# Layer 3's softmax totals in a four-layer graph-attention kernel: weights added up by fours on DVE, with one group of tile matmuls per head

## The chip, the cores and the metric

The kernel runs on one core of a Trainium2 chip. The metric is the device time of one launch, in microseconds (us), as a median over runs. The engines are named as in the profile: PE (TensorE matmul), PEld (its weight loads), DVE (VectorE), ACT (ScalarE), POOL (GpSimd) and SP (SyncE, which here issues DMAs). Each engine works through its own queue in order; where an instruction needs the result of another engine, it waits for a semaphore.

## The reference

There are 16 batches of 1024 nodes with 256 features, in fp32, and a 0/1 adjacency matrix per batch. Four attention layers follow one another. Each adds its result to x:

```python
h = jnp.maximum(_layernorm(x, axis=-1), 0.0)
x = x + _L3_gnn_ref(h, adj, ...)          # layers 0 to 2 likewise
```

Each layer projects h with a weight matrix, builds a 1024 x 1024 matrix of weights from two scores per node (masked by the adjacency), and takes the weighted mean of the projected values: the sum of weight times value over the source nodes, divided by the sum of the weights. Layer 3 does so with 4 heads of 64 features each, and then normalizes every head:

```python
dst = jnp.einsum('bhij,bhje->bhie', attention, h) + bias[None, :, None, :]
out = jax.nn.relu(dst) + h
out = (out - mu) / jnp.sqrt(var + EPS) * ln_gamma[...] + ln_beta[...]
```

The divisor of the softmax, one number per target node and head, is what the change computes in another way. It is called the total below.

## The kernel before, in words

**Streams.** The kernel keeps two batches under way. `stream(0)` runs the even batches, `stream(1)` the odd ones. Both are Python generators that emit instructions and yield planned times; the loop at the end of `short_path` always advances the stream whose planned time is behind, and stream 1 starts with a lag of 111 planned units. The order in which instructions are emitted is their precedence. A scheduler then fixes each engine's queue: where an instruction isn't ready by the scheduler's own account, a later one that is ready may go ahead. `keep_in_program_order` and `high_priority` pin some of them.

**A block** is 128 nodes; a batch has 8 (NI). Pairs of blocks are normalized and projected in `project`: the shifted relu (`center_by_sums`, L302, on DVE) makes `centered`, PE transposes it (L338), ACT copies it out (L340), PE multiplies with W (L345), and an evict function writes the values V (L413 to L417). The variance comes from a Square with accumulation on ACT (L309).

**Weights.** `weigh` fills a row of 1024 scores in PSUM by PE (L374 or L574) and makes for each source block j one 128 x 1024 tile of weights on DVE (L367), masked by the adjacency. A stream has 8 buffers for these tiles, and the two streams share the one row in PSUM.

**Layers 0 to 2** (`attend`) multiply with the weights as the stationary operand: for a target block, 8 matmuls over the source blocks into one accumulator of 257 columns (L461), whose last column is the total. `finish` then updates x_b (L385 to L397, or L501) on DVE and ACT.

**Layer 3** turns this around. The values of one head (64 columns, as two slices of 32) and a column for the total are the stationary operand, the weights of 512 targets the moving one. Each matmul uses a column tile of 32 (QUAD) columns of PE, and four of them, in four column tiles, make a group (`in_tiles`, L586). In `add_values` a source block takes four matmuls: two halves of the targets by two slices. In `add_totals` a pair of source blocks takes four: two halves by two blocks, with the total's column (E) broadcast to 32 columns. So a head has 32 matmuls for values and 16 for totals. Every fp32 matmul stands as two records in the trace, so these are 64 and 32 records. While head h is multiplied, DVE makes the weights of head h + 1.

After a head, ACT copies the two accumulators (L663), PE turns them (L670, L678), DVE takes the inverse of the totals and writes y (L672, L681). `center` (L544 to L556) adds the bias, relu and h3, and removes the mean; `rescale` (L560 to L562) multiplies with the inverse root of the variance and gamma and adds x. y is a buffer of its own, 8 KB per partition, from which the output is sent.

The lines that do the totals before:

```python
parts = [
    (V3[:, j + n, h, E:].to_broadcast([P, QUAD]), halves_of(h, j + n)[g])
    for g, n in ((0, 1), (0, 0), (1, 1), (1, 0))
]
in_tiles(parts, total, j == 2, j == NI - 4)
```

Of the kernel before, what the change touches and what calls it, by code (L numbers as in the profile page):

```python
# [41 lines left out]
P = 128  # L42
# [19 lines left out]
def short_path(ctx: ExitStack, tc: tile.TileContext, ins: dict, out: bass.AP, bad: bass.AP):  # L62
# [233 lines left out]
    def accumulator(b: int) -> bass.AP:  # L296
        return psum.tile([P, HALF], F32, name=f"acc{b % 2}")

    def center_by_sums(xb: bass.AP, minus_mean: bass.AP, pair: int, centered: bass.AP) -> bass.AP:

        for n in range(2):
            nc.vector.tensor_scalar(  # L302
                centered[:, n, :], xb[:, 2 * pair + n, :], minus_mean[:, n : n + 1], 0.0,
                op0=ALU.add, op1=ALU.max,
            )
        squared = small.tile([P, 2], F32, name="squared")
        for n in range(2):
            square = work.tile([P, D], BF, name="square", bufs=1)
            nc.scalar.activation(  # L309
                square, xb[:, 2 * pair + n, :], AF.Square, bias=minus_mean[:, n : n + 1],  # L310
                accum_out=squared[:, n : n + 1],
            )
        return inverse_root(squared, 2, D, LN_EPS)

    def project(b: int, l: int, xb: bass.AP, sums: bass.AP, pair: int, evict):


        centered = work.tile([P, 2, D], F32, name="centered", bufs=3)
        if sums is None:
            mv = small.tile([P, 2, nc.vector.BN_AGGR_DIM], F32, name="mv", bufs=2)  # L320
            for n in range(2):
                stats = small.tile([P, nc.vector.BN_STATS_DIM], F32, name="stats", bufs=1)
                nc.vector.bn_stats(stats, xb[:, 2 * pair + n, :])
                nc.vector.bn_aggr(mv[:, n, :], stats)
                nc.vector.tensor_scalar(  # L325
                    centered[:, n, :], xb[:, 2 * pair + n, :], mv[:, n, 0:1], 0.0,
                    op0=ALU.subtract, op1=ALU.max,
                )
            rstd = inverse_root(mv[:, :, 1], 2, D, LN_EPS, D)
        else:  # L330
            minus_mean = small.tile([P, 2], F32, name="minus_mean")
            nc.vector.tensor_scalar_mul(minus_mean, sums[:, ts(pair, 2)], -1.0 / D)  # L332
            rstd = center_by_sums(xb, minus_mean, pair, centered)
        yield 0.5
        turned = psum.tile([P, NK, 2 * P], F32, name="misc")
        for n in range(2):
            for k in range(NK):
                nc.tensor.transpose(turned[:, k, ts(n, P)], centered[:, n, ts(k, P)], ident)  # L338
        hT = wide.tile([P, NK, 2 * P], F32, name="hT", bufs=3)
        nc.scalar.mul(hT, turned, ROOT_D)  # L340
        yield 1.0
        for n in range(2):
            projected = accumulator(b)[:, : D + EXT[l]]
            for k in range(NK):
                nc.tensor.matmul(  # L345
                    projected, hT[:, k, ts(n, P)], W[l][:, k, :],
                    start=(k == 0), stop=(k == NK - 1),
                )
            evict(2 * pair + n, projected, rstd[:, n : n + 1])
        yield 2.5  # L350
# [25 lines left out]
    def start(behind, b: int):  # L376

        for t in behind:
            if row_taken == [b]:
                return  # L380
            yield t
# [19 lines left out]
    def batch(b: int):  # L401
# [130 lines left out]


        h3, ex = last["h3"], last["ex"]
        y = single.tile([P, NI, H, E], F32, name="y")
        normed = []

        def center(h: int, blocks=slice(0, NI), engine=nc.gpsimd):
# [19 lines left out]
        def rescale(yh: bass.AP, blocks, head, rstd: bass.AP, engine=nc.gpsimd):  # L558
            shape = list(yh.shape)
            nc.vector.tensor_mul(yh, yh, rstd.unsqueeze(2).to_broadcast(shape))  # L560
            engine.tensor_mul(yh, yh, gamma[:, head].unsqueeze(1).to_broadcast(shape))
            engine.tensor_add(yh, yh, xb[:, blocks, head])  # L562

        weights = []

# [27 lines left out]
        def halves_of(h: int, j: int):  # L593
            return [weights[h * NI + j][:, ts(g, HALF)] for g in range(NH)]
# [8 lines left out]
                ]  # L603
                in_tiles(parts, acc, n == 3, n == NI - 4)

        def add_totals(h: int, j: int):

            parts = [
                (V3[:, j + n, h, E:].to_broadcast([P, QUAD]), halves_of(h, j + n)[g])
                for g, n in ((0, 1), (0, 0), (1, 1), (1, 0))  # L610
            ]
            in_tiles(parts, total, j == 2, j == NI - 4)

        behind = weigh3(0)
        yield from start(behind, b)

        rest = small.tile([P, NI, H], F32, name="rest", bufs=1)
        nc.gpsimd.tensor_scalar_mul(rest, ex[:, :, 2 * H :], THIRDS)
# [2 lines left out]
        nc.gpsimd.tensor_sub(rest, rest, thirds[:, 0])  # L621
        nc.gpsimd.tensor_copy(thirds[:, 1], rest)
        nc.gpsimd.tensor_sub(thirds[:, 2], rest, thirds[:, 1])
        for h in range(H):


            acc = accumulator(b)
            total = accumulator(b)
            if h == 0:
                for first in range(0, NI, 4):  # L630
                    for _ in range(4):
                        next(behind)
                    pinned = []
                    for j in (first + 2, first):
                        add_values(h, j)
                    yield 3.6
                for _ in behind:
                    pass
                turned_thirds = psum.tile([3 * QUAD, P], BF, name="misc")
                made = nc.tensor.transpose(  # L640
                    turned_thirds, thirds.rearrange("p t i h -> p (t i h)"), ident_bf
                )
                tc.keep_in_program_order(made)
                thirds_T = small.tile([3 * QUAD, P], BF, name="thirds_T", bufs=1)
                nc.scalar.copy(thirds_T, turned_thirds)
            behind = weigh3(h + 1)
            yield from start(behind, b)

            for first in range(0, NI, 4):
                pinned = []  # L650
                for j in (first + 2, first):
                    add_totals(h, j)
                    if h > 0:
                        add_values(h, j)
                for _ in range(4):
                    next(behind, None)
                yield 1.8 if h == 0 else 5.4
            for _ in behind:
                pass
            copies = []  # L660
            for accT in (acc, total) if h == 0 else (total, acc):
                copies.append(wide.tile([P, HALF], F32, name="sums"))
                nc.scalar.copy(copies[-1], accT)  # L663
                next(testing)
                next(coming, None)
            sums, totals = copies if h == 0 else copies[::-1]
            yield 0.5
            turned = psum.tile([P, NG, P], F32, name="misc")
            for i in range(NG):
                nc.tensor.transpose(turned[:, i, :], totals[:, ts(i, P)], ident)  # L670
            inv = small.tile([P, NH, NG], F32, name="inv8", bufs=3)
            nc.vector.tensor_reduce(  # L672
                inv, turned[:, :, ::QUAD].rearrange("p i (g n) -> p g i n", n=2), AX.X, ALU.add
            )
            inverse(inv, inv)
            turned = psum.tile([P, NG, NH, E], F32, name="misc")
            for i in range(NG):
                nc.tensor.transpose(  # L678
                    turned[:, i].rearrange("p g e -> p (g e)"), sums[:, ts(i, P)], ident
                )  # L680
            nc.vector.tensor_mul(  # L681
                y[:, :, h, :].rearrange("p (g i) e -> p g i e", g=NH),
                turned.rearrange("p i g e -> p g i e"),
                inv.unsqueeze(3).to_broadcast([P, NH, NG, E]),
            )
            yield 0.5
            if h > 0:
                rescale(*normed.pop())


            if b < B - 1:
                normed.append(center(h))
            elif h < H - 1:
                normed.append(center(h, engine=nc.gpsimd if h < H - 2 else nc.vector))
            else:
                normed += [center(h, slice(g * NG, g * NG + NG), nc.vector) for g in range(NH)]
            yield 1.0
        for _ in coming:
            pass
        while normed:  # L700
            rescale(*normed.pop(0), engine=nc.vector if len(normed) == 0 and b == B - 1 else nc.gpsimd)
        for g in range(NH):
            queue = nc.gpsimd if b < B - 1 else (nc.sync, nc.scalar)[g]
            queue.dma_start(
                in_blocks(out[b, ts(g, HALF), :]),
                y[:, ts(g, NG)].rearrange("p (c t) h e -> p c t (h e)", t=2),
            )
        yield 1.0

# [395 lines left out]
```

## Time and profile before

| | |
|---|---|
| median of 3 runs | 2933.43 us (2932.90 to 2933.43) |
| profiled execution, its own time | 2933.13 us |
| profiled span | 2931.4 us |
| mean granted TensorE clock | 0.995 |
| PE busy | 2810.0 us, 96% |
| DVE busy | 2147.9 us, 73% |
| ACT busy | 1088.2 us, 37% |
| POOL busy | 981.3 us, 33% |
| tile matmuls of layer 3 (L586) | 6144 records, 691.7 us |
| DVE weights of layer 3 (L367 from ex) | 512, mean 1272 ns |
| shifted relu on DVE (L302) | 504, 195.7 us |

The profile describes one execution. A busy time is the union of an engine's instructions, so a share near 100% says that the engine was rarely empty, and not yet that it set the pace: the chain of work that ended last, followed back from the end, tells who was waited for. The mean of a group can be longer than its step in the queue, since instructions overlap at their ends; four tile matmuls even run at once. The windows of the trace give busy times for one stretch, and are the way to tell one stage from another.

### The profile page before, as it was taken

Reading aid. Unit: us, or ns where it says so; the run is one execution under the profiler, and the core shown is the slowest. Engines: PE = TensorE matmul, PEld = TensorE weight load, DVE = VectorE, ACT = ScalarE, POOL = GpSimd, SP = SyncE. Lnnn points to the kernel's source line nnn. Section 1 sums busy time; section 2 is a strip of 40 time slices with the busy share of each in tenths; the row PEclk is TensorE's granted clock in tenths of the full one; section 3 lists DMA queues with packets and bytes.
Section 4 is the critical chain, followed back from the end, with each engine's and each line's share of the span. In section 5 each row is a group of like instructions: output and inputs, shape, how many; then the busy total and the mean of one; then the engine's idle time right before and its main releaser. Section 6 shows DMA issues by size and latency. Waiting matters only on the chain.

```text
span 2931.4 us, 44756 instructions
## 1 busy us (share of the span) xinstructions
PE 2810.0 (96%) x16790; PEld 1961.9 (67%) x16790; DVE 2147.9 (73%) x4490; ACT 1088.2 (37%) x3010; POOL 981.3 (33%) x1533
## 2 busy tenths in 40 slices
PE   7999999999999999999999999999999999999986
PEld 5775857668576685766758577685766857667552
DVE  5658688586976859778586885868768587685857
ACT  1333434343343433424334343433434334343332
POOL 2123324243242423424233242432424224242333
PEclk9999999999999999999999999999999999999998
DMA  8204022030321303122031220303203031110101
GB/s 126 39 8 65 30 30 58 8 51 29 37 51 16 56 17 51 37 29 59 1 51 37 30 58 8 51 30 37 51 12 47 29 49 39 15 30 1 22 22 31
DMA packets 127967, 106.14 MB, mean 36 GB/s; under 512 B 79872, under 2 KB 98432, under 8 KB 127744
## 3 DMA queue, kind: packets, MB, share of 16 engines
q0 software_dynamic: 47328, 66.10, 15.4%
q1 hardware_dynamic: 79568, 35.53, 5.4%
q8 instruction: 135, 2.21, 0.3%
q10 hardware_dynamic: 848, 1.57, 0.2%
q14 instruction: 88, 0.72, 0.1%
HBM read 153.49 MB, written 33.55 MB: 64 GB/s over the span
## 4 chain that ended last, share of the span: by engine, by line
PE 59%; DVE 26%; issue 8%; POOL 3%; ACT 3%; DMA 0%; POOLq 0%; ACTq 0%; SPq 0%; DVEq 0%
PE acc L461 36%; DVE weights L367 16%; PE acc L586 10%; PE acc L345 9%; PE misc L338 2%; DVE centered L302 2%; POOL rstd L293 2%; DVE V L417 1%; PE row L374 1%; POOL y L544 1%; DVE y L545 1%; DVE var L555 1%; ACT square L309 1%; DVE y L551 1%; DVE mean L549 1%
## 5 line engine op out<-in xcount | busy, mean ns | idle before, releaser
L461 PE MATMUL acc<-V,weights 128*128 128x257 f32 x6144 | 1435.6, 384 | 33.5 <-DVE weights L367 15.7
L461 PEld LDWEIGHTS acc<-V,weights 128*128 128x128 f32 x6144 | 1136.6, 190 | 281.9 <-DVE weights L367 75.3
L586 PE MATMUL acc<-weights,V 128*32 128x512 f32 x6144 | 691.7, 596 | 12.0 <-DVE weights L367 8.1
L367 DVE SCALAR_TENSOR_TENSOR weights<-row,ex,mask 128x1024 f32<-128x1024 f32 x512 | 629.0, 1272 | 97.3 <-PE row L574 65.8
L345 PE MATMUL acc<-W,hT 128*128 128x259 f32 (+1 forms) x2048 | 516.1, 389 | 38.1 <-ACT hT L340 26.9
L367 DVE SCALAR_TENSOR_TENSOR weights<-row,V,mask 128x1024 f32<-128x1024 f32 x384 | 473.7, 1273 | 0.8 <-PE row L374 0.8
L345 PEld LDWEIGHTS acc<-W,hT 128*128 128x128 f32 x2048 | 378.7, 190 | 135.1 <-ACT hT L340 44.4
L586 PEld LDWEIGHTS acc<-weights,V 128*32 128x32 f32 x6144 | 189.1, 110 | 417.7 <-issue 410.3
L393 ACT ACTIVATE below<-acc,inv 128x256 f32<-128x256 f32 x256 | 121.1, 473 | 813.1 <-DVE inv L386 569.6
L293 POOL TENSOR_TENSOR rstd<-rstd,minus_half 128x2 f32<-128x2 f32 (+1 forms) x321 | 292.8, 912 | 20.3
L309 ACT ACTIVATE square<-x_b,minus_mean 128x256 bf16<-128x256 f32 x504 | 255.7, 507 | 110.3 <-DVE minus_mean L332 105.3
L441 POOL TENSOR_TENSOR x_b<-x_b,beta 128x256 f32<-128x256 f32 x128 | 93.5, 731 | 488.6 <-ACT square L309 483.5
L292 POOL TENSOR_SCALAR rstd<-squared 128x2 f32<-128x2 f32 x252 | 80.0, 317 | 464.0 <-ACT square L309 451.0
L385 DVE TENSOR_SCALAR inv<-acc 128x1 f32<-128x1 f32 x256 | 39.1, 153 | 255.3 <-PE acc L461 254.0
L302 DVE TENSOR_SCALAR centered<-x_b,minus_mean 128x256 f32<-128x256 f32 x504 | 195.7, 416 | 5.1
L340 ACT ACTIVATE hT<-misc 128x512 f32<-128x512 f32 x256 | 150.2, 592 | 129.6 <-PE misc L338 129.3
L396 DVE SCALAR_TENSOR_TENSOR x_b<-below,x_b 128x256 f32<-128x256 f32 x256 | 131.8, 515 | 84.9 <-ACT below L393 83.0
L663 ACT COPY sums<-acc 128x512 f32<-128x512 f32 x128 | 74.9, 585 | 308.6 <-PE acc L586 301.0
L413 ACT ACTIVATE V<-acc,rstd 128x3 f32<-128x3 f32 x384 | 98.4, 261 | 231.1 <-PE acc L345 230.6
L417 DVE TENSOR_SCALAR V<-acc,rstd,V 128x256 f32<-128x256 f32 x256 | 131.4, 537 | 59.8 <-ACT V L413 58.9
L338 PE MATMUL misc<-ident,centered 128*128 128x128 f32 x1024 | 158.7, 277 | 13.7 <-DVE centered L325 11.5
L170 POOL DMA_DIRECT2D adj_i<-in_adj_dram x128 | 74.4, 582 | 290.1 <-ACT adj_i L175 248.8
(96 smaller groups left out, 2212.8 us busy)
## 6 DMA issues: line engine op xcount, KB each, us to landing
adj_i<-in_adj_dram POOLq DMA_DIRECT2D x128, 256.0 KB, 3.9
x_b<-in_x_dram SPq DMA_DIRECT2D x15, 1024.0 KB, 6.4
narrow<-in_adj_dram POOLq DMA_DIRECT2D x60, 256.0 KB, 9.3
out_dram<-y POOLq DMA_DIRECT2D x30, 512.0 KB, 7.5
x_b<-in_x_dram ACTq DMA_DIRECT2D x4, 256.0 KB, 6.1
narrow_half<-in_adj_dram POOLq DMA_DIRECT2D x4, 256.0 KB, 16.9
mask<-narrow SPq DMA_TRANSPOSE x60, 3.7
weights<-in_L_gnn_a_dram SPq DMA_DIRECT2D x3, 256.0 KB, 5.5
```

The source lines that it names most:

```text
L293: nc.gpsimd.tensor_tensor(r, r, minus_half.to_broadcast([P, n]), op=ALU.pow)
L302: nc.vector.tensor_scalar(centered[:, n, :], xb[:, 2 * pair + n, :], minus_mean[:, n : n + 1], 0.0, op0=ALU.add, op1=ALU.max,)
L309: nc.scalar.activation(square, xb[:, 2 * pair + n, :], AF.Square, bias=minus_mean[:, n : n + 1], accum_out=squared[:, n : n + 1],)
L338: nc.tensor.transpose(turned[:, k, ts(n, P)], centered[:, n, ts(k, P)], ident)
L340: nc.scalar.mul(hT, turned, ROOT_D)
L345: nc.tensor.matmul(projected, hT[:, k, ts(n, P)], W[l][:, k, :], start=(k == 0), stop=(k == NK - 1),)
L367: nc.vector.scalar_tensor_tensor(w, r, c(j), masks[b][:, j // 2, :, j % 2], op0=op, op1=ALU.mult)
L393: nc.scalar.activation(below, acc[:, :D], AF.Exp, scale=inv)
L396: nc.vector.scalar_tensor_tensor(xi, below, 1.0, xi, op0=ALU.min, op1=ALU.add)
L417: nc.vector.tensor_scalar(V[:, i, :D], projected[:, :D], rstd, V[:, i, D : D + 1], op0=ALU.mult, op1=ALU.mult,)
L461: nc.tensor.matmul(accs[i], weights[j][:, ts(i, P)], V[:, j, : D + 1], start=(j == 0), stop=(j == NI - 1),)
L586: made = nc.tensor.matmul(accT[ts(n, QUAD), :], values, moving, start=first, stop=last)
```

## The change

Layer 3's totals are made in two steps. `add_up` adds the weights of four source blocks into one 128 x 1024 tile (`added`, two buffers) on DVE. The blocks' total columns differ from node to node, so each step multiplies what has been added so far with the ratio of two neighbouring blocks' columns (`ratio`), and the last block's column is left for PE. `add_totals` then needs one group per head: four matmuls, two halves by two tiles of four blocks. It stands behind the first values of the next head, and the closing of a head (copies, transposes, inverse, y, center, rescale) moves with it, into a function `close` that runs within the next head's loop. The planned times in layer 3 change with that.

Three smaller parts: in layers 1 to 3 the shifted relu is an ACT activation instead of a DVE instruction; y lies in V3, whose values are no longer needed once a head has been multiplied; and the last addition of `rescale` writes into x_b, from which the output is now sent.

```diff
-    def center_by_sums(xb: bass.AP, minus_mean: bass.AP, pair: int, centered: bass.AP) -> bass.AP:
+    def center_by_sums(
+        l: int, xb: bass.AP, minus_mean: bass.AP, pair: int, centered: bass.AP
+    ) -> bass.AP:
         for n in range(2):
-            nc.vector.tensor_scalar(
-                centered[:, n, :], xb[:, 2 * pair + n, :], minus_mean[:, n : n + 1], 0.0,
-                op0=ALU.add, op1=ALU.max,
-            )
+            x_n, mean_n = xb[:, 2 * pair + n, :], minus_mean[:, n : n + 1]
+            if l > 0:
+                nc.scalar.activation(centered[:, n, :], x_n, AF.Relu, bias=mean_n)
+            else:
+                nc.vector.tensor_scalar(
+                    centered[:, n, :], x_n, mean_n, 0.0, op0=ALU.add, op1=ALU.max
+                )
...
-        y = single.tile([P, NI, H, E], F32, name="y")
+        y = V3[:, :, :, :E]
...
-            engine.tensor_add(yh, yh, xb[:, blocks, head])
+            engine.tensor_add(xb[:, blocks, head], yh, xb[:, blocks, head])
...
-        def add_totals(h: int, j: int):
+        added, totals_of = {}, {}
+
+        def add_totals(h: int):
             parts = [
-                (V3[:, j + n, h, E:].to_broadcast([P, QUAD]), halves_of(h, j + n)[g])
-                for g, n in ((0, 1), (0, 0), (1, 1), (1, 0))
+                (V3[:, 4 * c + 3, h, E:].to_broadcast([P, QUAD]), added[h, 4 * c][:, ts(g, HALF)])
+                for g in range(NH)
+                for c in range(NI // 4)
             ]
-            in_tiles(parts, total, j == 2, j == NI - 4)
+            in_tiles(parts, totals_of[h], True, True)
+
+        def add_up(h: int, first: int):
+            s = added[h, first] = single.tile([P, N], F32, name="added", bufs=2)
+            for j in range(first + 1, first + 4):
+                w = weights[h * NI + j]
+                before = weights[h * NI + first] if j == first + 1 else s
+                nc.vector.scalar_tensor_tensor(
+                    s, before, ratio[:, j, h : h + 1], w, op0=ALU.mult, op1=ALU.add
+                )
...
+        ratio = ex[:, :, :H]
+        nc.vector.reciprocal(ratio, ratio)
+        nc.gpsimd.tensor_mul(ratio[:, 1:], ratio[:, 1:], V3[:, : NI - 1, :, E])
...
+        closing = iter(())
+        for h in range(H):
+            acc = accumulator(b)
+            if h > 0:
+                behind = weigh3(h + 1)
+                yield from start(behind, b)
+            for first in range(0, NI, 4):
+                if h == 0:
+                    for _ in range(4):
+                        next(behind)
+                pinned = []
+                for j in (first + 2, first):
+                    add_values(h, j)
+                if first == 0 and h > 0:
+                    totals_of[h - 1] = accumulator(b)
+                    add_totals(h - 1)
+                    closing = close(*to_close)
+                add_up(h, first)
+                if h > 0:
+                    for _ in range(4):
+                        next(behind, None)
+                    yield 2.7
+                    yield from closing
+                    closing = iter(())
+                    yield 2.0
+                else:
+                    yield 3.6
...
-                y[:, ts(g, NG)].rearrange("p (c t) h e -> p c t (h e)", t=2),
+                xb[:, ts(g, NG), :].rearrange("p (c t) f -> p c t f", t=2),
```

For head 0 the loop differs in one thing: its weights are made in front of its values, and head 1's weights after it, as before. The last head's totals and its closing follow the loop.

More of the change, by code (lines that the diff above doesn't have):

```diff
@@ L332, in project @@
             nc.vector.tensor_scalar_mul(minus_mean, sums[:, ts(pair, 2)], -1.0 / D)
-            rstd = center_by_sums(xb, minus_mean, pair, centered)
+            rstd = center_by_sums(l, xb, minus_mean, pair, centered)
         yield 0.5
@@ L623, in batch, with copy_of, close @@
         nc.gpsimd.tensor_sub(thirds[:, 2], rest, thirds[:, 1])
[L624 to L666, printed above, removed]
+        def copy_of(accT: bass.AP) -> bass.AP:
+            copied = wide.tile([P, HALF], F32, name="sums")
+            nc.scalar.copy(copied, accT)
+            next(testing)
+            next(coming, None)
+            return copied
+        def close(h: int, sums: bass.AP):
+            totals = copy_of(totals_of.pop(h))
             yield 0.5
@@ L686, in batch @@
             yield 0.5
-            if h > 0:
+            if normed:
                 rescale(*normed.pop())
@@ L695, in batch @@
             else:
-                normed += [center(h, slice(g * NG, g * NG + NG), nc.vector) for g in range(NH)]
+                normed.extend(
+                    center(h, slice(g * NG, g * NG + NG), nc.vector) for g in range(NH)
+                )
             yield 1.0
+        closing = iter(())
[25 more added lines that the diff above has]
+                    yield 3.6
+            for _ in behind:
+                pass
+            sums = copy_of(acc)
+            if h == 0:
+                turned_thirds = psum.tile([3 * QUAD, P], BF, name="misc")
+                made = nc.tensor.transpose(
+                    turned_thirds, thirds.rearrange("p t i h -> p (t i h)"), ident_bf
+                )
+                tc.keep_in_program_order(made)
+                thirds_T = small.tile([3 * QUAD, P], BF, name="thirds_T", bufs=1)
+                nc.scalar.copy(thirds_T, turned_thirds)
+                behind = weigh3(1)
+                yield from start(behind, b)
+                for _ in range(2):
+                    for _ in range(4):
+                        next(behind)
+                    yield 1.8
+                for _ in behind:
+                    pass
+            to_close = h, sums
+        pinned = []
+        totals_of[H - 1] = accumulator(b)
+        add_totals(H - 1)
+        yield from close(*to_close)
         for _ in coming:
```

## The prediction

> **What bounds the kernel now.** I read the page first (shares and slices), then the chain, then the groups. A group's mean over the whole kernel hides its stages, so I went on to the windows of one steady cycle and to the timelines of PE and DVE inside it.
>
> ```profile
> PE 2810.0 (96%) x16790; PEld 1961.9 (67%) x16790; DVE 2147.9 (73%) x4490; ACT 1088.2 (37%) x3010; POOL 981.3 (33%) x1533
> PE 59%; DVE 26%; issue 8%; POOL 3%; ACT 3%; DMA 0%; POOLq 0%; ACTq 0%; SPq 0%; DVEq 0%
> ```
>
> PE looks full, but a quarter of the chain runs through DVE: in some stage PE is paced by DVE. The groups that the change touches:
>
> ```profile
> L586 PE MATMUL acc<-weights,V 128*32 128x512 f32 x6144 | 691.7, 596 | 12.0 <-DVE weights L367 8.1
> L367 DVE SCALAR_TENSOR_TENSOR weights<-row,ex,mask 128x1024 f32<-128x1024 f32 x512 | 629.0, 1272 | 97.3 <-PE row L574 65.8
> L302 DVE TENSOR_SCALAR centered<-x_b,minus_mean 128x256 f32<-128x256 f32 x504 | 195.7, 416 | 5.1
> L309 ACT ACTIVATE square<-x_b,minus_mean 128x256 bf16<-128x256 f32 x504 | 255.7, 507 | 110.3 <-DVE minus_mean L332 105.3
> ```
>
> Layer 3's first weights appear on DVE every 178.5 us (1090.8, 1269.3): one batch per cycle, from the two streams in turn. I cut a cycle in two: the stretch in which one batch is in layer 3, to its last rescale (L560), and the rest, in which both streams are in layers 0 to 2. Columns: us, then busy us of PE, PEld, DVE, ACT, POOL, each with its records.
>
> ```profile
> 1090.80:1195.90 105.10, 101.65 (x701) 60.43 (x699) 90.01 (x162) 42.76 (x112) 37.85 (x50) 1.00 0.30 41
> 1195.90:1269.30 73.40, 72.85 (x352) 62.02 (x351) 43.41 (x116) 25.40 (x77) 23.70 (x46) 1.00 0.10 29
> ```
>
> The next cycle repeats these numbers. In the rest PE is full and DVE has 30 us free. In layer 3's stretch both are near their limit, DVE with 15 us free in 105. Its densest part, from another cut of the windows:
>
> ```profile
> 1110.00:1130.00 20.00, 19.34 (x142) 9.78 (x142) 19.64 (x25) 4.95 (x11) 5.72 (x8) 1.00 0.32 49
> 1130.00:1145.00 15.00, 14.44 (x95) 8.83 (x93) 14.49 (x28) 3.61 (x10) 5.34 (x7) 1.00 0.79 71
> ```
>
> DVE reaches 34.1 of 35 us there, 97.5%. PE's timeline prices the tile groups, DVE's the weights:
>
> ```profile
> 1139.84 5.36 PE L586 MATMUL acc<-weights,V 128*32 128x512 f32 x48
> 1106.44 9.62 DVE L367 SCALAR_TENSOR_TENSOR weights<-row,ex,mask 128x1024 f32<-128x1024 f32 x8 [3.87 <-PE row L574]
> ```
>
> In the chain 48 such records take 5.29 us, 0.110 each, since four column tiles run side by side. Eight weights take 9.6 us of DVE, 1.20 each.
>
> **What the Trainium skill says.** "TensorEngine Tiling (Array Packing)", Tiling Modes: at 128x32 four tiles run independently; the 0.110 us per record beside 0.217 for a whole-array record (16 of L461 in 3.47 us) agrees, though the trace cannot separate the drain that the page sets on a change of mode. "VectorE: DVE Perf Modes", Why `tensor_tensor` can't do 2×_2P or 4×: two tensors in fp32 get one element per cycle. The trace agrees for scalar_tensor_tensor: L397 follows itself at 0.34 us for 256 elements, L545 at 0.60 for 512, 1.0 ns per element. "SBUF — State Buffer", Who interferes with whom: DVE with two SBUF inputs and a GpSimd instruction that reads SBUF lock each other out. L396 and L397 (medians 0.42 us) have outliers of 1.5 and 1.3 us, which fits. L367 reads the row from PSUM; the new additions have both tensors in SBUF. "TensorE: Matmul & The Clock Gate", Architectural detail: ACT and DVE are strict first-in first-out, so a waiting addition holds all of DVE's later work.
>
> **The change, part by part, for one batch.**
>
> *Totals on PE.* Before, a head has 32 matmuls of values and 16 of totals; after, 32 and 4. Two records each: 24 records fewer per head, 96 per batch. 96 x 0.110 = 10.6 us less PE, all in layer 3's stretch.
>
> *Additions on DVE.* Two add_up per head with three instructions each: 24 per batch, 384 in all, 128x1024 fp32. No row shows this form. Lower bound 0.60 + 512 x 0.001 = 1.11 us, L545's step stretched to 1024. Upper: two of each three wait for the one before, and L396 to L397 on the same tile takes 0.53 us where independent ones take 0.34, so +0.19; with 0.1 for POOL's lock, 1.4. I take 1.27, L367's mean: 30.5 us per batch (bounds 26.6 and 33.6).
>
> *relu on ACT.* 24 of a batch's 32 leave DVE at 195.7/504 = 0.388 us: 9.3 us. By the counts of L302 (18 in layer 3's stretch, of which I put 8 down to the next batch's layer 0, that stay), 10 leave that stretch, 3.9 us. On ACT 24 x 0.5 (L309) = 12 us, where it is 41% busy: nothing on the path. The transposes L338 wait for relu; a neighbour's block of 3.47 us lies ahead of them on PE and hides the about 0.4 us by which two relus end later. If this cover is gone: 12 pairs x 0.4 = 4.8 us per batch.
>
> *y in V3, output from x_b.* L562 writes elsewhere, in the same number. The output DMAs now hold x_b instead of y; they land in 7.5 us, and x_b has three buffers, and by the code the next fetch into this one is issued near the end of the next batch's layer 3, some 70 us after: nothing. If that cover is gone, at most 7.5 us per batch.
>
> *ratio.* A reciprocal and a POOL product of 128x32: about 0.3 us each. *Order.* Yields in layer 3 sum to 50 instead of 53, so the other stream gets no more work in this stretch than before.
>
> *New waits.* Only two `added` buffers: the next head's first addition waits until PE has run four blocks' values (32 records, 3.5 us) and the totals (8, 0.9 us). Behind it on DVE stand the next weights and the other stream's evictions, and PE waits for both. Weights 4 to 7 on DVE (4.8 us) lie ahead of it and cover 4.4. In return the additions fill DVE's wait for the next row (3.87 us above).
>
> *Sum for layer 3's stretch.* DVE: 90.0 + 30.5 - 3.9 + 0.3 = 116.9 us; at 97.5% that needs 119.9, so +14.8. PE has 101.65 - 10.6 = 91.0 in it, thus some 29 us free: what PE saves here isn't waited for any longer. Can work from the rest fill it? Each us of PE work from there brings 43.41/72.85 = 0.60 us of DVE work, into a full DVE. x us moved shorten the cycle by x - 0.6x/0.975 = 0.39x. The traced order gives the older work, layer 3's, the precedence on DVE, so I take x = 10, about three blocks of 3.47: -3.9. The cycle grows by 10.9 us. Fifteen such are 163.5. The last batch runs layer 3 alone: 30.5 more DVE work, of which some 8 fit into the row wait before head 1 (7.90 us in its timeline) and some 4 into other gaps: +18. Total +181.5 on the profiled execution's 2933.1 (span 2931.4, 1.7 outside; the median of the runs is 2933.4, the same within 0.3 us): 3115 us.
>
> **Rivals.**
>
> *Half hidden:* x of 20 to 38, because the next batch's layer 0 already starts inside layer 3's stretch (its sums, L517, stand at 1145 on DVE). +7 down to 0 per batch: 2940 to 3055, middle 3000. Against it: those carry DVE work too.
>
> *Faster, the load spreads:* over 38 us (14.8/0.39), more than half of the rest's 72.85, moves into layer 3's stretch, so PE becomes the only bound again. For it: DVE's total would be 133.4 + 30.5 - 9.3 = 154.6 us in a cycle, still under PE's 174.5 - 10.6 = 163.9, so no sum forbids it. Against: the yields move nothing that way. At x = 55 the cycle loses 6.6 us: 15 x -6.6 + 18 gives 2852; PE's own bound is 16 x -10.6, 2763.
>
> *A wait in place of the work:* a foreign block (16 of L461, 3.47 us) stands before the values on PE, so the addition waits 4.4 + 3.5 - 4.8 = 3.1 us, for three heads: 9.3 per batch, 3115 + 149 = 3264 at worst. For it: PE's timeline has such blocks between the groups of L586. Against: PE now has time to spare there.
>
> **How the numbers follow.** Main case (x up to 20, 3055 to 3173) 0.52; half hidden 0.20; the wait 0.12; faster 0.13; no change 0.03. 0.2% is about what a measurement of this kernel tells from no change. Slower is 0.52 + 0.20 + 0.12 = 0.84. The range of 2905 to 3200 leaves out about 0.10 below, most of the faster case, and 0.09 above, most of the wait; the bounds of an addition's price, -3.9 and +3.1 us per batch before the moved work, lie within. The likeliest case alone: 3055 to 3173.
>
> **What would show it.** Tile matmuls 4608 records instead of 6144, PE's busy sum about 2640. A new DVE row of 384 at 1.1 to 1.4 us; DVE busy 2148 + 488 - 149, about 2490. ACT about 1280. Layer 3's stretch near 120 us with DVE over 95% and PE under 90%; the rest still near 70 and full on PE. DVE's share of the chain over 35%. I'm wrong if the cycle is 178 us or less, with other layers' blocks filling PE in layer 3; or if DVE shows idle time in front of the additions, released by tile matmuls; or if transposes wait for relu on ACT in the rest.

## The result

The changed kernel takes 3400.65 us (3391.6 to 3405.1) against 2933.43: a ratio of 1.159, interval 1.156 to 1.161. That is slower, as forecast, but by 467 us where 182 were forecast, and outside the range.

The page of the changed kernel: the busy shares, two rows of slices, and the groups that answer to those of before (L586 is now L592, L367 is L372, L302 is L306 on ACT).

```profile
PE 2879.4 (85%) x15254; PEld 1980.1 (58%) x15254; DVE 2476.2 (73%) x4506; ACT 1250.9 (37%) x3394; POOL 1080.2 (32%) x1549
...
PE   7977998889888798878989799897998979988774
...
PEclk9988998989999899999999899998998989999887
...
L592 PE MATMUL acc<-weights,V 128*32 128x512 f32 x4096 | 550.8, 686 | 208.6 <-DVE weights L372 188.2
L372 DVE SCALAR_TENSOR_TENSOR weights<-row,ex,mask 128x1024 f32<-128x1024 f32 x512 | 629.0, 1275 | 24.1 <-PE row L580 18.0
...
L306 ACT ACTIVATE centered<-x_b,minus_mean 128x256 f32<-128x256 f32 x384 | 177.2, 503 | 487.2 <-DVE minus_mean L337 486.6
L629 DVE SCALAR_TENSOR_TENSOR added<-added,ex,weights 128x1024 f32<-128x1024 f32 x256 | 341.9, 1336 | 0.1
...
L629 DVE SCALAR_TENSOR_TENSOR added<-weights,ex,weights 128x1024 f32<-128x1024 f32 x128 | 170.6, 1339 | 13.6 <-PE acc L592 13.6
```

No engine is full now: PE 85%, DVE 73%. PE stands idle 208.6 us ahead of the values of layer 3, where it was 12.0 ahead of values and totals together. The granted clock has holes that it didn't have.

The starts of layer 3, read from its first weights on DVE, lay 178.5 us apart before. Now they alternate: 234.1 and 179.1 us in the middle of the run, 413.2 for two batches instead of 357.0. The same two stretches as before, cut again at the first weights on DVE and at the last rescale, for two batches in turn (columns as before: us, busy PE, PEld, DVE, ACT, POOL, clock, DMA):

```profile
1038.10:1165.70 127.60, 98.17 (x577) 57.19 (x575) 112.46 (x171) 43.23 (x111) 43.26 (x44) 0.91 0.25 34
1165.70:1272.20 106.50, 102.77 (x482) 84.92 (x483) 57.52 (x138) 43.06 (x127) 29.37 (x60) 0.98 0.17 30
1272.20:1386.50 114.30, 92.12 (x537) 50.96 (x537) 104.93 (x153) 39.09 (x96) 37.42 (x36) 0.91 0.17 28
1386.50:1451.30 64.80, 63.87 (x314) 54.36 (x314) 32.02 (x99) 31.39 (x94) 25.21 (x52) 1.00 0.10 33
```

Layer 3's stretch takes 121.0 us on average (105.1 before), the rest 85.7 (73.4 before). So the rest, too, has become longer, although the change itself adds no work to it.

What PE waits for, by the waits of its own queue, in the kernel before and in the changed one (us, times, longest):

```profile
PE acc L461 <- DVE weights L367: 15.7, 20, 2.7
...
PE acc L586 <- DVE weights L367: 8.1, 4, 5.0
```

```profile
PE acc L592 <- DVE weights L372: 188.2, 47, 12.3
PE acc L592 <- DVE added L629: 49.1, 18, 5.1
PE acc L466 <- DVE weights L372: 43.0, 39, 1.6
PE acc L350 <- ACT above L400: 33.5, 15, 5.0
```

One such wait from near: PE's timeline, and DVE's at the same time.

```profile
1105.28 0.61 PE L580 MATMUL row<-thirds_T,rows_of 96*128 96x128 bf16 x8
1112.85 5.57 PE L592 MATMUL acc<-weights,V 128*32 128x512 f32 x32 [6.96 <-DVE weights L372]
1118.24 1.02 PE L592 MATMUL acc<-added,V 128*32 128x512 f32 x2
```

```profile
1105.55 1.27 DVE L629 SCALAR_TENSOR_TENSOR added<-added,ex,weights 128x1024 f32<-128x1024 f32 x1
1106.75 1.28 DVE L372 SCALAR_TENSOR_TENSOR weights<-row,ex,mask 128x1024 f32<-128x1024 f32 x1
1107.94 1.28 DVE L629 SCALAR_TENSOR_TENSOR added<-added,ex,weights 128x1024 f32<-128x1024 f32 x1
1109.13 3.66 DVE L372 SCALAR_TENSOR_TENSOR weights<-row,ex,mask 128x1024 f32<-128x1024 f32 x3
```

DVE doesn't pause here, and PE waits 7 us for four weights, ahead of and between which two additions stand. After the wait the 32 records take 5.57 us, where 32 took 3.64 before: the clock was halved meanwhile (the lines are in the last section).

### The profile page after: what moved, and what is told of

It reads as the page before. It is cut to its first block, busy times and chain, and to the rows that moved or that the text cites. A ratio compares the mean times of both kernels' runs of the same rounds, so it can differ in the third digit from the quotient of the medians.

```text
span 3396.5 us, 41828 instructions
## 1 busy us (share of the span) xinstructions
PE 2879.4 (85%) x15254; PEld 1980.1 (58%) x15254; DVE 2476.2 (73%) x4506; ACT 1250.9 (37%) x3394; POOL 1080.2 (32%) x1549
## 5 line engine op out<-in xcount | busy, mean ns | idle before, releaser
L466 PE MATMUL acc<-V,weights 128*128 128x257 f32 x6144 | 1470.7, 390 | 59.0 <-DVE weights L372 43.0
L466 PEld LDWEIGHTS acc<-V,weights 128*128 128x128 f32 x6144 | 1154.9, 194 | 332.5 <-DVE weights L372 111.6
L592 PE MATMUL acc<-weights,V 128*32 128x512 f32 x4096 | 550.8, 686 | 208.6 <-DVE weights L372 188.2
L372 DVE SCALAR_TENSOR_TENSOR weights<-row,ex,mask 128x1024 f32<-128x1024 f32 x512 | 629.0, 1275 | 24.1 <-PE row L580 18.0
L350 PE MATMUL acc<-W,hT 128*128 128x259 f32 (+1 forms) x2048 | 549.1, 407 | 87.8 <-ACT above L400 33.5
L350 PEld LDWEIGHTS acc<-W,hT 128*128 128x128 f32 x2048 | 385.8, 197 | 212.1 <-ACT hT L345 59.7
L372 DVE SCALAR_TENSOR_TENSOR weights<-row,V,mask 128x1024 f32<-128x1024 f32 x384 | 469.2, 1275 | 29.6 <-PE row L379 29.3
L592 PEld LDWEIGHTS acc<-weights,V 128*32 128x32 f32 x4096 | 138.5, 123 | 542.8 <-issue 383.2
L306 ACT ACTIVATE centered<-x_b,minus_mean 128x256 f32<-128x256 f32 x384 | 177.2, 503 | 487.2 <-DVE minus_mean L337 486.6
L629 DVE SCALAR_TENSOR_TENSOR added<-added,ex,weights 128x1024 f32<-128x1024 f32 x256 | 341.9, 1336 | 0.1
L293 POOL TENSOR_TENSOR rstd<-rstd,minus_half 128x2 f32<-128x2 f32 (+1 forms) x321 | 332.5, 1036 | 20.2
L398 ACT ACTIVATE below<-acc,inv 128x256 f32<-128x256 f32 x256 | 121.0, 473 | 567.7 <-DVE inv L391 383.6
L345 ACT ACTIVATE hT<-misc 128x512 f32<-128x512 f32 x256 | 149.4, 595 | 148.4 <-PE misc L343 148.3
L343 PE MATMUL misc<-ident,centered 128*128 128x128 f32 x1024 | 162.7, 284 | 24.6 <-ACT centered L306 11.5
L629 DVE SCALAR_TENSOR_TENSOR added<-weights,ex,weights 128x1024 f32<-128x1024 f32 x128 | 170.6, 1339 | 13.6 <-PE acc L592 13.6
```

The source lines that it names most:

```text
L293: nc.gpsimd.tensor_tensor(r, r, minus_half.to_broadcast([P, n]), op=ALU.pow)
L306: nc.scalar.activation(centered[:, n, :], x_n, AF.Relu, bias=mean_n)
L350: nc.tensor.matmul(projected, hT[:, k, ts(n, P)], W[l][:, k, :], start=(k == 0), stop=(k == NK - 1),)
L372: nc.vector.scalar_tensor_tensor(w, r, c(j), masks[b][:, j // 2, :, j % 2], op0=op, op1=ALU.mult)
L398: nc.scalar.activation(below, acc[:, :D], AF.Exp, scale=inv)
L466: nc.tensor.matmul(accs[i], weights[j][:, ts(i, P)], V[:, j, : D + 1], start=(j == 0), stop=(j == NI - 1),)
```

## The experiments

The theory was A: DVE's load in layer 3's stretch is the cost. The rivals were B (the new order of layer 3 is), C (relu on ACT comes late for PE) and D (y in V3 brings waits).

**Without the additions.** The totals' matmuls read a tile of ones.

```diff
-                (V3[:, 4 * c + 3, h, E:].to_broadcast([P, QUAD]), added[h, 4 * c][:, ts(g, HALF)])
+                (V3[:, 4 * c + 3, h, E:].to_broadcast([P, QUAD]), all_ones[:, ts(g, HALF)])
...
-                add_up(h, first)
```

> The changed kernel, with the additions on DVE left out: the four tile matmuls of the totals read a constant tile of ones, so the totals are not the reference's, and all else, order and yields too, is as in the changed kernel. Theory A, DVE's load in layer 3's stretch: 30 us of DVE per batch go away, PE's 10.6 us per batch stay saved, so the time falls below the kernel before, to 2770 to 2900 us, with PE's granted clock back at 0.99. Theory B, the new order of the closing and the smaller yields starve PE: it stays above 3150 us.

Measured: 2969.1 us, ratio 1.012 (1.011 to 1.014), clock 0.976. The additions are worth 432 us, which speaks for A. But the time lies in neither range: DVE now has less to do than before the change, PE too, and the kernel is still 36 us slower than before. A isn't all.

**relu back on DVE**, in the changed kernel.

```diff
-            if l > 0:
+            if l > 3:
```

> The changed kernel with the shifted relu of layers 1 to 3 back on DVE. Theory A: DVE gets 9.3 us per batch more, some 4 of them in layer 3's stretch, so 3420 to 3500 us. Rival C, relu on ACT comes late and starves the transposes on PE in the rest of the cycle: it gets faster, 3250 to 3380 us.

Measured: 3436.6 us, ratio 1.171 (1.169 to 1.173). As A expected: relu on ACT helps by 36 us here.

**relu on ACT alone**, in the kernel before: the same lines of `center_by_sums` as in the change.

> The kernel before with only the shifted relu of layers 1 to 3 on ACT. Theory A: DVE loses 4 us in layer 3's stretch, where it is nearly full, so 2880 to 2930 us. Rival C, the relu on ACT is late for PE: 2940 to 3000 us.

Measured: 3003.4 us, ratio 1.023 (1.022 to 1.025). Here C's number nearly came out (3 us above its range): 70 us slower, though DVE is busy 100 us less. The waits of this run don't show C's mechanism, however. The transposes' group, L341 here, waited 0.4 us for relu on ACT. What grew is PE's wait for an accumulator that ACT still has to read, from 5.4 us, and for one that DVE reads once ACT has written its part of V, from 5.3 us (second fence: the kernel before):

```profile
PE acc L348 <- ACT above L398: 31.9, 36, 2.2
PE acc L348 <- DVE V L420: 23.6, 14, 1.7
```

```profile
PE acc L345 <- ACT above L395: 5.4, 24, 0.5
PE acc L345 <- DVE V L417: 5.3, 14, 0.4
```

The likely reason, argued and not tested, is that the relus now stand ahead of these steps in ACT's queue. The two waits are 45 of the 70 us; the remainder was not traced.

**y in V3 alone**, in the kernel before.

```diff
-        y = single.tile([P, NI, H, E], F32, name="y")
+        y = V3[:, :, :, :E]
...
-            engine.tensor_add(yh, yh, xb[:, blocks, head])
+            engine.tensor_add(xb[:, blocks, head], yh, xb[:, blocks, head])
```

> The kernel before with only y in V3's columns and the output sent from x_b. Theory A: no engine gets more work, 2925 to 2945 us. Rival D, y's writes into V3 and the longer hold of V3 and x_b bring new waits between heads: over 2960 us.

Measured: 2931.05 us, ratio 0.999 (0.998 to 1.000). D falls.

**The additions alone, in the old order**, their sums unused.

```diff
...
+                add_up(h, first)
                 for _ in range(4):
                     next(behind, None)
                 yield 1.8 if h == 0 else 5.4
```

> The kernel before (with y in V3, which makes the room) plus the additions on DVE alone, behind each half head's matmuls and ahead of the next weights; their sums are not used, the totals are made on PE as before. Theory A, DVE's load in layer 3's stretch is what costs: with no PE work saved and relu still on DVE, at least as slow as the changed kernel less the order's part, 3250 to 3500 us. Theory B, the new order of layer 3 is the larger part: the additions fit into DVE's idle time to a good part, 2950 to 3150 us.

Measured: 3280.1 us, ratio 1.118 (1.116 to 1.120): 349 us above y in V3 alone, for 384 additions (and the ratio's two small instructions per batch), 0.91 us each. In the old order, too, most of an addition's 1.28 us is paid for. A holds. The starts of layer 3 stay even, about 200 us apart, and DVE is busy 94% of the stretch:

```profile
1201.70:1325.60 123.90, 105.33 (x692) 60.40 (x691) 116.65 (x187) 42.44 (x111) 42.12 (x47) 0.94 0.26 35
```

Every run with additions has them ahead of the next weights in DVE's queue. How much of their cost is DVE's load, and how much the delay of those weights, was not separated.

**Without the additions, relu on DVE:** the first two edits together.

> The changed kernel without the additions (constant ones in their place, totals not the reference's) and with relu on DVE: what is left is the new order of layer 3, the new yields, y in V3 and the 12 matmuls fewer per head. If relu on ACT costs the same here as alone (70 us): 2885 to 2920 us. If relu on ACT helps wherever DVE is busy in layer 3: 2975 to 3010 us.

Measured: 3021.8 us, ratio 1.030 (1.029 to 1.032). Nearest to the second case, 12 us above its range: in the new order relu on ACT gains 53 us. What is left of the change here saves PE work and adds only the ratio's two small instructions, and it costs 3%.

**A quarter of the totals, in the old order**, on ones again, with y in V3.

```diff
+            if j != 2:
+                return
...
-            in_tiles(parts, total, j == 2, j == NI - 4)
+            in_tiles(parts, total, True, True)
```

> The kernel before in its own order, with 4 instead of 16 matmuls of totals per head, reading a constant tile of ones (the totals are not the reference's), and y in V3. Theory A': PE sets the pace over the whole cycle, 10.6 us per batch are worth their full price: 2760 to 2830 us. Rival: layer 3's stretch is DVE's already, what PE saves there isn't waited for: 2890 to 2932 us.

Measured: 2873.7 us, ratio 0.980 (0.978 to 0.981). Between the two: of 170 us of PE work, 57 are gained over y in V3 alone. The price list of the idea is thus 349 us for additions against 57 for matmuls. And between this run and the one before lie 148 us that come from the new loop of layer 3, for the same work but for the ratio.

**Larger yields**, in the changed kernel.

```diff
-                    yield 2.7
+                    yield 5.0
                     yield from closing
                     closing = iter(())
-                    yield 2.0
+                    yield 5.0
...
-                    yield 3.6
+                    yield 6.0
...
-                    yield 1.8
+                    yield 3.6
```

> The changed kernel with larger planned times in layer 3 (5.0 and 5.0 in place of 2.7 and 2.0, 6.0 for 3.6, 3.6 for 1.8), so that the other stream emits about 1.9 times as much work beside layer 3. Theory B, the order starves PE of other layers' blocks in that stretch: faster, 3150 to 3330 us. Theory A alone, DVE is full there whatever the order: 3360 to 3440 us.

Measured: 3304.8 us, ratio 1.127 (1.125 to 1.129). B's range: what the other stream emits beside layer 3 is worth 96 us even with the same load on DVE. Two cycles of this run, cut as above:

```profile
1023.10:1161.40 138.30, 111.58 (x638) 67.11 (x637) 124.00 (x185) 47.37 (x117) 48.38 (x58) 0.93 0.30 39
1161.40:1202.50 41.10, 38.23 (x183) 30.16 (x182) 24.08 (x58) 19.52 (x62) 18.44 (x38) 1.00 0.14 51
1202.50:1331.90 129.40, 112.08 (x662) 70.77 (x661) 114.34 (x195) 47.87 (x127) 39.66 (x44) 0.93 0.14 25
1331.90:1423.80 91.90, 88.98 (x431) 74.30 (x431) 45.14 (x119) 41.10 (x120) 26.23 (x53) 1.00 0.07 24
```

Layer 3's stretch takes 133.9 us on average and the rest 66.5: here other layers' work did move into layer 3's stretch, and the cycle is 200.4 us.

**The lag**, in the changed kernel.

```diff
-    LAG = 111.0
+    LAG = 108.0
```

> The changed kernel with a lag of 108 planned units in place of 111 (half of the new planned sum of a batch, 215.7). Theory B1, the two streams' uneven offset is a cost (layer 3 starts 234 and 179 us apart): the starts get even and the time falls to 3310 to 3380 us. Rival: the offset is a sign, not a cost: 3385 to 3415 us.

Measured: 3321.1 us, ratio 1.132 (1.130 to 1.134). The starts of layer 3 now lie an even 201.4 us apart, and 80 us are gained by one number.

**The same lag without the additions** and with relu on DVE.

> The run with no additions and relu on DVE (3021.8 us), with a lag of 108. B1: most of the order's 148 us comes from the uneven offset (211 and 157 us apart): 2880 to 2950 us. Rival B2, it is the placing of totals and closing behind the next head, or the smaller yields: 2990 to 3030 us.

Measured: 3000.0 us, ratio 1.022 (1.021 to 1.024). B2's range, and only 22 us of the 148: here the uneven offset is mostly a sign.

**The old planned sum without the additions** and with relu on DVE.

```diff
-                    yield 2.7
+                    yield 3.4
...
-                    yield 2.0
+                    yield 2.7
```

> The run with no additions and relu on DVE (3021.8 us), with 3.4 and 2.7 in place of 2.7 and 2.0, so that a batch's planned sum is the old 219.9 and the lag fits. If the smaller planned times (offset and share) are the order's cost: 2870 to 2950 us. If the placing of totals and closing behind the next head's values is: 2990 to 3030 us.

Measured: 3096.2 us, ratio 1.056 (1.054 to 1.057): 74 us slower, which neither expectation had. A planned sum that fits the lag isn't enough. A likely reason, not tested, is that with the closing moved behind the next head the same sum puts other instructions side by side.

**PE's work given back**, in the changed kernel.

```diff
-            in_tiles(parts, totals_of[h], True, True)
+            for _ in range(4):
+                in_tiles(parts, totals_of[h], True, True)
```

> The changed kernel with each group of totals run four times over (every run starts the sum anew, so the result is the same): PE has the old number of tile matmuls, DVE the additions. Theory A, PE waits in layer 3's stretch, so its saving there isn't waited for: 3390 to 3440 us. Rival: PE's work still counts fully, 10.6 us per batch: 3530 to 3590 us.

Measured: 3406.3 us, ratio 1.161 (1.159 to 1.163): 6 us for 12 matmuls more per head, 768 in all. In the changed kernel PE's saving is worth next to nothing, since PE waits in that stretch anyway. Two effects are mixed here, though: the granted clock rises from 0.931 to 0.953. By the clock records of the two traces, PE was busy at half clock for 360 us in the changed kernel and for 270 us here, so the better clock gave back at most 45 of the 170 us of work that were added.

**Totals and closing at once**, without the additions and with relu on DVE: they stand right after the head's own values, as before the change.

```diff
-                if first == 0 and h > 0:
-                    totals_of[h - 1] = accumulator(b)
-                    add_totals(h - 1)
-                    closing = close(*to_close)
...
-            to_close = h, sums
-        pinned = []
-        totals_of[H - 1] = accumulator(b)
-        add_totals(H - 1)
-        yield from close(*to_close)
+            pinned = []
+            totals_of[h] = accumulator(b)
+            add_totals(h)
+            yield from close(h, sums)
```

> The run with no additions and relu on DVE (3021.8 us), with each head's totals and closing right after its own values, as in the kernel before, and not behind the next head's first values. If that placing is the order's cost: 2870 to 2920 us (the quarter of totals in the old order took 2873.7). If not: 2980 to 3040 us.

Measured: 2969.4 us, ratio 1.012 (1.010 to 1.014). Between the two ranges: the placing is 52 of the 148 us. Layer 3 starts evenly again, with no change of the lag.

**The same edit in the changed kernel**, with its additions.

> The changed kernel, additions and relu on ACT included, with each head's totals and closing right after its own values. PE then waits for the head's last additions. If the placing is the order's cost: 3230 to 3330 us. If PE's wait for the additions outweighs it: 3410 to 3550 us.

Measured: 3307.0 us, ratio 1.127 (1.126 to 1.129). 94 us less. PE's wait for the additions grows from 49.1 to 68.6 us in all, and costs less than the placing behind the next head, which spares PE a part of it.

**The misfit of the lag in the kernel before.**

```diff
-    LAG = 111.0
+    LAG = 113.1
```

> The kernel before with a lag of 113.1 in place of 111, the same misfit to half of its planned sum as the changed kernel has. If an uneven offset costs in itself: 2950 to 3010 us. If it costs only where DVE is overloaded: 2925 to 2940 us.

Measured: 3054.5 us, ratio 1.041 (1.039 to 1.043). No instruction is added or removed, and the time grows by 120 us, more than either case; layer 3's starts alternate between 195 and 177 us. The order of the two streams is by itself worth 4% here. Other lags of the kernel before were not tried.

**Closing at once, with the old planned times**, without the additions and with relu on DVE, and then with both.

```diff
                     yield 2.7
-                    yield from closing
-                    closing = iter(())
-                    yield 2.0
+                    yield 2.7
```

> The run with closing at once and no additions (2969.4 us), with 2.7 and 2.7 in place of 2.7 and 2.0: every planned time of layer 3 is that of the kernel before. If placing and planned times together are the order's whole cost: 2865 to 2890 us, as the quarter of totals (2873.7). If something else of the new loop costs: 2930 us or more.

> The changed kernel, additions and relu on ACT included, with closing at once and all planned times of the kernel before. The additions alone cost 349 us in the old order; less some 60 for PE's work, plus or minus relu on ACT (-36 to +70): 3180 to 3290 us. If the additions' cost doesn't depend on the order: 3300 to 3350 us.

Measured: 2932.7 us, ratio 0.9995 (0.999 to 1.000), and 3256.9 us, ratio 1.110 (1.108 to 1.112): the second case of the one, the first of the other. Another 37 and 50 us are planned times. With both taken back 59 us remain to the 2873.7 of the old loop; what of the new loop costs them was not found. The two still differ in that the totals and their copy follow the values instead of preceding them, and in the ratio; neither was tested alone. Two cycles of the second run:

```profile
1189.60:1311.50 121.90, 99.14 (x594) 57.22 (x592) 113.13 (x176) 45.07 (x117) 40.34 (x45) 0.96 0.27 35
1311.50:1386.80 75.30, 74.58 (x360) 63.97 (x361) 40.86 (x104) 32.71 (x98) 25.32 (x53) 1.00 0.08 29
1386.80:1507.60 120.80, 99.61 (x594) 56.59 (x593) 113.27 (x176) 45.25 (x117) 40.34 (x45) 0.94 0.26 35
1507.60:1582.80 75.20, 74.55 (x360) 63.93 (x361) 40.75 (x103) 32.65 (x98) 25.21 (x53) 1.00 0.09 29
```

3256.9 is the best that was reached with the additions in it: still 11% slower than before. No version with the reference's totals beats the kernel before by more than y in V3's 0.1%.

The way from 2933.3 to 3400.7, one part after the other by neighbouring runs:

| step | runs compared | us |
|---|---|---|
| y in V3 | 2933.3, 2931.1 | -2 |
| 12 of 16 totals' matmuls fewer per head, old order | 2931.1, 2873.7 | -57 |
| new loop of layer 3: placing 52, planned times 37, unexplained 59 | 2873.7, 3021.8 | +148 |
| relu on ACT, in the new order | 3021.8, 2969.1 | -53 |
| additions on DVE, in the new order | 2969.1, 3400.7 | +432 |

The parts depend on each other: in the old order the additions alone cost 349 and relu on ACT alone +70.

## Why the prediction was wrong

*Totals on PE.* The count was right, 4096 + 512 = 4608 records, and that little of the saving would be felt: 57 of 170 us in the old order, 6 beside the additions.

*Additions on DVE.* 30.5 us per batch forecast, 31.1 and 32.7 measured in the two stretches. The median is 1.28 us. The mean of 1.34 comes from 34 of the 384 that take over 1.3 us, up to 2.4; POOL is at work beside each of them, as the Trainium skill ("SBUF — State Buffer", Who interferes with whom) lets one expect where POOL reads SBUF. POOL's last addition went from 1300 to 1693 ns; with y in V3 alone it didn't grow. The 0.19 us for an addition that needs the one before didn't show: the 20 such pairs with nothing between them follow each other at 1.19 us, like weights. DVE's busy sum was 2476 for 2490 forecast. (Two readings of the prediction were loose: the steps of 0.34 and 0.60 us are those from an L397 or L545 to whatever comes next on DVE, and the Trainium skill's rate for two fp32 tensors stands in the perf-mode tier table of "VectorE: DVE Perf Modes", a section ahead of the one named.)

*DVE's filling: the first step that failed.* I let DVE fill layer 3's whole stretch to 97.5%. That share came from its densest 35 us; in the prediction's own window of the whole stretch DVE was busy 90.0 of 105.1 us, 86%. Measured are 88 and 92%, and no window of the stretch that is shown here exceeds 94%. In the first of the two stretches DVE stood idle for 15 us, of which 4.4 were for POOL's bias addition (L550), 3.7 for POOL's inverse root (L293) and 3.7 for PE's accumulators: steps that hand work from engine to engine, and that a sum of busy times doesn't see.

*The moved work: the second.* I took x = 10 us of other layers' PE work as moved into layer 3's stretch. About 8 moved out. Records in the stretch before and, on average of the two, after: L461 148 and 137, L345 60 and 43, L338 36 and 24, L374 16 and 8. At 0.22 us each for the first two and 0.11 for the others these are 2.4 + 3.8 + 1.3 + 0.9 = 8.4 us. The prediction had the sign at hand: smaller planned times let the other stream emit less beside layer 3, not more. (They fell by 4.2 for a batch, six times 5.4 against 2.7 and 2.0, not by the 3 of "50 instead of 53".)

*What each is worth.* The cycle grew by 28.1 us, not by 10.9. By the prediction's own exchange of 0.39 us, 18 us of x are 7 of the 17.2 that are missing. Another 6 are DVE's filling: with x = -8 and 97.5% layer 3's stretch would have taken 114.8 us, and it took 121.0. The last 4 lie in the rest, 81.8 with that x and 85.7 measured, by clock (0.98 in one of two) and idle PE (2.3 us, 0.6 before). Fifteen cycles make 258 of the 285 us that are missing. The last batch alone grew from 83.7 us (last row from ex to the end) to 114.9, by 31 for 18.

Two runs bear this out. With the larger yields x was +11, about as forecast, and the rest took 66.5 us (63.4 forecast). But layer 3's stretch took 133.9 where 126.0 were forecast, with DVE at 90 and 88%, and the run took 3304.8 us: the larger yields, with the forecast x, took off only 96 of the 285 us. With closing and planned times of before (3256.9 us) x was -2, DVE at 93 and 94%, and the cycle still grew by 18 us.

*Order: costed at nothing.* I had costed the smaller yields and the moved closing at nothing, because the other stream would get "no more work". That the order of two streams has a price of its own I didn't ask. With the additions it is 144 us, from 3400.7 to 3256.9, and 6 of the 18 us by which x was wrong; the other 12 stay in the order of before. Without the additions it is 148 us, 59 of them of unknown cause, and in the kernel before 120 us for 2.1 planned units of lag.

*relu on ACT.* Costed at nothing with a neighbour's block as its cover. The cover held: the transposes waited 0.4 us for relu where it was moved alone, 11.5 us in the changed kernel. But alone it cost 70 us, 45 of them in two waits behind ACT's later steps: I asked who waits for relu, and not what stands behind it in ACT's queue. In the changed kernel it gains 36 us; that DVE is the scarcer there fits, but wasn't tested apart.

*y in V3* was right at nothing.

*The wait for the two added buffers* was a rival with 149 us. DVE waited 13.6 us in all ahead of the first additions for PE. It falls; the other way round, PE waited 49.1 us for the additions.

*What would show it.* PE's busy sum was to be 2640 and is 2879: records stretched at half clock, for at most 180 us, and beside waits (L592 at 686 ns, 596 before). The chain can't be read: in this page it covers only some 4% of the span. The rest was to stay near 70 us (63.4 by the main case's own sum); that it grew is the sign I had not named.

## What to carry to other kernels

Take the share to which an engine can fill a stretch from the whole stretch, with its waits in it, and not from its densest part: 97.5% against some 90% was as costly here as work that moved the wrong way. Where two streams share in-order queues, the stretch in which one of them crowds an engine also decides how far the other gets: ask which way work moves, into the fuller stretch or out of it, before its sign goes into a sum. Before one reads a change's cost from busy times, the order should be tested by itself, with a number that changes no work: a lag moved by 2 units cost 4% here, more than many changes. And an exchange of matmuls for vector additions pays only by the price that each has in its stage: 57 us for the one and 349 for the other, far from their busy times of some 170 and 510.

## What the runs showed of the hardware

PE's granted clock fell to half in pieces of layer 3: it was 0.931 on average (0.995 before), and 0.91 in both stretches of layer 3. Around the wait shown above (columns as before; the clock is the third number from the end):

```profile
1105.89:1110.00 4.11, 0.00 (x0) 0.00 (x0) 4.11 (x4) 0.00 (x0) 0.00 (x0) 0.99 0.00 0
1110.00:1112.85 2.85, 0.00 (x0) 0.00 (x1) 2.85 (x6) 0.00 (x0) 0.00 (x0) 0.50 0.00 0
1112.85:1116.30 3.45, 3.45 (x20) 0.82 (x24) 3.45 (x8) 1.57 (x4) 2.53 (x2) 0.50 0.00 0
1116.30:1119.26 2.96, 2.96 (x23) 0.69 (x15) 2.96 (x10) 0.00 (x0) 1.48 (x1) 0.92 0.00 0
```

It fell 4 us after PE's last matmul and stayed at half for about the first 4 us of the next ones. 32 records of tile matmuls then took 5.57 us; in the kernel before they took 3.64:

```profile
1146.60 3.64 PE L586 MATMUL acc<-weights,V 128*32 128x512 f32 x32
```

In all, PE was busy at half clock for 360 us in the changed kernel and for 9 us before. So at most 180 us of PE's time are the clock's. How much of that reached the kernel's time was not separated: with totals repeated the clock rose to 0.953 and the time changed by 6 us.

DVE's additions, with both tensors in SBUF, took 1.28 us (median) and up to 2.4 us, the long ones always beside a POOL instruction. The 512 weights of layer 3, which read one tensor from PSUM, stayed at 1.29 us or less in the same trace.
